# Grouping the scan's products of two slots, and reordering the work between two Mamba layers

## The chip, the cores and the metric

The kernel runs on one core of a Trainium2 chip. The metric is the device time of one launch in microseconds (us). A core has a matrix engine (TensorE, PE, with its weight loads as PEld), a vector engine (VectorE, DVE), a scalar engine for activations (ScalarE, ACT), a general engine (GpSimd, POOL), and a queue that issues the DMAs (SyncE, SP). Each engine works through its own list of instructions in order; semaphores tie the lists together.

## The reference

The network takes four images of 256 channels and 64 x 64 positions in float32 and applies four layers to each. The first two are recurrent and windowed attention layers, which the change does not touch. The third is a Mamba layer over the 4096 positions: a layer norm, a projection to 512 channels and a gate of 512, a causal convolution of four taps, SiLU, and then for each channel a state of 16 numbers that is carried along the sequence:

```python
def step(h, inp):
    d_t, u_t, B_t, C_t = inp
    dA = jnp.exp(d_t[..., None] * A)
    h = dA * h + (d_t * u_t)[..., None] * B_t[:, None, :]
    y_t = jnp.einsum('bdn,bn->bd', h, C_t)
    return (h, y_t)
```

After that come y + u * D, the gate silu(z), an output projection and a sum into x (with statistics of x that the next layer's norm uses). The fourth layer is a grouped Mamba: a layer norm over 256 channels, four groups of 64 channels that share one Mamba of 128 inner channels, a small MLP with GELU per group, a 1 x 1 convolution with batch norm, and SiLU; its result is added to x and written out.

## The kernel before, in words

The four images run one after the other: attention_layers, mamba_layer (the first Mamba layer) and grouped_mamba_layer (the second). The image x stays in SBUF.

Both Mamba layers use scan_blocks (L907). The sequence is cut into four chunks of 1024 positions (NC), and a chunk into four blocks of 128 channels, so there are 16 blocks. A block has 16 slots, one for each number n of the state, 256 slots per layer and image. For one slot i:

- spread (L937 to L951): PE copies row n of B over all 128 partitions into a PSUM tile pb (two bf16 matmuls of 512 columns against a picking column).
- L1019: DVE multiplies pb by du = delta * u, in place.
- decay (L954, L961): ACT computes da = exp(delta * a_n).
- L1025: DVE's scan instruction runs h = da * h + pb along the 1024 positions.
- L1031: POOL multiplies h by C (cb, loaded by DMA with a broadcast) into hc.
- turn (L969, L977): PE adds hc into y with eight transposes, which accumulate in PSUM over the 16 slots.

Some slots are "apart": n = 0, 5, 10 in the first layer, 0, 4, 8 in the second. There B is loaded by DMA (bb), POOL makes the product (L935), and ACT writes the exponentials into PSUM (dap). The tag pb has two PSUM buffers, which pb and dap take in turn, so what belongs to slot i + 2 can be written only when the scan of slot i has ended.

The order is written out by hand. For slot i the loop issues: the product of slot i, the scan, POOL's product of slot i + 2 if that is apart, hc, decay(i + 3), the loads, then background steps, spread(i + 2), further background steps (n + 0.5), turn(i - 1), and the exponentials of slot i + 2 if that is apart. Background steps come from a table per block (blk["bg"], filled by put): input projections (u_ps, z_ps), SiLUs, x_proj (tables of B and C), delta, norms, output projections and the MLP, each at a fixed slot. Each engine meets these in the order of issue. end (L985) finishes a block during the next one: a copy of y, transposes back, the D term (fin_ps), and the gate product (L991).

Between the layers, for each image (L1539 to L1587): a function center is called by scan_blocks after its last slot and ahead of the last turn. It computes the next norm's means (L1544) and subtracts them (L1548). Then follow the last output products (L1392), squares (L1561 and L863), sums over the channels (L1572 for the norm's variance, L817 for the statistics of x), a short chain on DVE, and the reciprocal root. In the second layer come the scaling, a first product, constants (skip, f1b, wf1, bns, bnb, L1923 to L1945), the folded convolution weights (folds, L1214, on the results of small matmuls at L1209), the first convolution on DVE (evict and convolve, L1895 to L1910), the SiLU of the first block, x_proj and delta, and then scan_blocks.

Of the kernel before, what the change touches and what calls it, by code (L numbers as in the profile page):

```python
# [8 lines left out]
F32 = mybir.dt.float32  # L9
# [3 lines left out]
ALU = mybir.AluOpType  # L13
# [5 lines left out]
P = 128  # L19
# [8 lines left out]
NT = 512  # L28
NC = 1024
# [15 lines left out]
class Net:  # L45
# [858 lines left out]

    def scan_blocks(self, blocks, loop, psum, psb, psy, apart, ends, first, last=None):  # L907
# [6 lines left out]

        def is_apart(i):
            return 0 < i < n_slot and slots[i][1] in apart

        def pieces(i):
            return halves if i == n_slot - 1 else [slice(0, NC)]
# [65 lines left out]
        def end(blk, n):  # L985
            if n == ends[0]:
                for ss in halves:
                    nc.scalar.activation(blk["du"][:, ss], blk["y"][:, ss], AF.Copy)
            for j, (ss, first) in enumerate(zip(halves, ends[1:])):
                if n == first + 1:  # L990
                    nc.vector.tensor_tensor(  # L991
                        blk["zs"][:, ss], blk["out", j], blk["zs"][:, ss], ALU.mult
                    )
# [21 lines left out]
            decay(i, True)  # L1015
            product(i)
        for i, (blk, n) in enumerate(slots):
            if not is_apart(i):
                nc.vector.tensor_tensor(pb[i], blk["du"], pb[i], ALU.mult)  # L1019
            h[i] = loop.tile([P, NC], F32, tag="h", name="h", bufs=3)  # L1020
            for ss in pieces(i):
                state = 0.0 if blk["first"] else blk["state"](n)
                if ss.start:
                    state = h[i][:, ss.start - 1 : ss.start]
                nc.vector.tensor_tensor_scan(  # L1025
                    h[i][:, ss], da[i][:, ss], pb[i][:, ss], state, ALU.mult, ALU.add
                )
# [12 lines left out]
            if i >= DS and n == ends[0]:  # L1040
                end(slots[i - DS][0], n)
            spread(i + 2)
            for step in blk["bg"].get(n + 0.5, ()):
                step()
            turn(i - 1)
            decay(i + 2, True)
            for d in (pb, da, cb):
                del d[i]
        if last:
            last()  # L1050
        turn(n_slot - 1)
        for n in range(ends[2] + 2):
            end(blocks[-1], n)


    def exp_ln_tables(self):
# [165 lines left out]
    def mamba_layer(self, x, bridge, pe_dram, w_in, w_cw, w_x, w_dt, w_out, v_dram):  # L1222
        tc, nc = self.tc, self.nc
        ND = 4
        with ExitStack() as ctx:
# [310 lines left out]
            xs3 = x.rearrange("p (c t) -> p c t", c=2)  # L1536


            def center():  # L1539
                nc.gpsimd.memset(xn[:, :, 0:3], 0.0)  # L1540
                pm = psb.tile([P, NC], F32, tag="pb", name="ln_pm")
                for ss in first:
                    for c in range(2):
                        nc.tensor.matmul(  # L1544
                            pm[:, ss], self.one_ln, xs3[:, c, ss], start=(c == 0), stop=(c == 1)
                        )
                for ss in first:
                    nc.vector.tensor_tensor(  # L1548
                        xn[:, :, 3 + ss.start : 3 + ss.stop], xs3[:, :, ss],
                        pm[:, ss].rearrange("p (o t) -> p o t", o=1).to_broadcast([P, 2, NT]),  # L1550
                        ALU.subtract,
                    )

            self.scan_blocks(
                [blk for c in chunks for blk in c["blocks"]], loop, psum, psb, psy, (0, 5, 10),
                (1, 2, 4), (xs0[4:6], (), xs0[6:]), center,
            )
            late_square, late_sums, late_squares, finish = late_stats
            sq3 = work.tile([P, 2, NC + 3], F32, tag="xn", name="ln_sq")
            for ss in first:  # L1560
# [5 lines left out]
            for s in range(2):  # L1566
                for m in range(2):
# [12 lines left out]
            wi = bridge.tile([P, 6, P], F32, tag="w2", name="m3_wi")  # L1580
            erow = self.eps_row(wi[:, 5, 0:S].rearrange("p (g t) -> p g t", t=2), finish())
# [22 lines left out]
    def grouped_mamba_layer(self, x, bridge, begun, ws_dram, outc_dram, v_dram, out_b, load):  # L1604
        tc, nc = self.tc, self.nc
        w_in, w_cw, w_x, w_dt, w_out, w_f1, w_f2 = ws_dram
        with ExitStack() as ctx:
# [136 lines left out]
            def delta(k, q):  # L1744
                return self.delta_steps(chunks[k]["blocks"][q], wdt, work, psum)
# [184 lines left out]
            f1b = wp.tile([P, 2], F32, name="m3_f1b")  # L1930
            pf = psum.tile([P, NT], F32, tag="mm", name="pf")
            for f in range(2):
                nc.tensor.matmul(
                    pf[:, f : f + 1], wf1[0:64, f * P : (f + 1) * P],
                    vec[0:64, M3_L1B : M3_L1B + 1], start=True, stop=True,
                )
            nc.vector.tensor_tensor(f1b, pf[:, 0:2], vec[:, M3_F1B : M3_F1B + 2], ALU.add)
            nc.vector.tensor_scalar(wf1, wf1, vec[:, M3_L1G : M3_L1G + 1], None, ALU.mult)
# [3 lines left out]
            nc.vector.tensor_tensor(bns, bns, vec[:, M3_BG : M3_BG + 2], ALU.mult)  # L1942
            bnb = wp.tile([P, 2], F32, name="m3_bnb")
            nc.vector.tensor_tensor(bnb, bns, vec[:, M3_BM : M3_BM + 2], ALU.mult)
            nc.vector.tensor_tensor(bnb, vec[:, M3_BB : M3_BB + 2], bnb, ALU.subtract)  # L1945
            for f in folds:
                f()
# [19 lines left out]
            for i, (k, c) in enumerate(pairs):  # L1967
                even, odd = chunks[k]["blocks"][2 * c : 2 * c + 2]

                def put(blk, where, steps):  # L1970
                    for i, f in zip(where, steps):
                        blk["bg"].setdefault(i, []).append(f)
# [7 lines left out]
                if more:  # L1980
# [5 lines left out]
                put(even, (4, 5, 9, 11, 12, 13), x_proj(k, 2 * c + 1))  # L1986
# [12 lines left out]
                put(even, (7, 9, 8, 9, 10), delta(k, 2 * c + 1))  # L1999
# [6 lines left out]
                put(even, (3,), (silu(k, c, "zs", also),))  # L2006
                if c == 1 and k:
                    put(even, (4, 5, 6, 7), [out(k - 1, *sm) for sm in outs])
                    put(even, (8,), [lambda k=k: load(slice((k - 1) * NC, k * NC))])
# [9 lines left out]
                    put(odd, (9, 11, 10, 11, 12), delta(nk, 2 * ncol))  # L2019
                    put(odd, (13, 14), [in_z(nk, ncol, s) for s in range(2)])  # L2020
            self.scan_blocks(
                [blk for c in chunks for blk in c["blocks"]], loop, psum, psb, psy, (0, 4, 8),
                (1, 2, 2), (xs0[2:4], (), xs0[4:]),
            )

# [161 lines left out]
```

## Time and profile before

| | us |
|---|---|
| median of three runs | 11817.76 |
| lowest and highest | 11803.92, 11832.72 |
| the profiled execution | 11811.95 |
| its span | 11810.1 |
| first Mamba loop, last image, first to last scan | 937 |
| between the layers, last image | 55 |
| second Mamba loop, last image | 956 |

| engine | busy share of the span |
|---|---|
| PE | 84% |
| DVE | 83% |
| POOL | 74% |
| ACT | 60% |

The span is cut from the profile's first to last instruction. Times on the timeline count from its start. In a line of the timeline the columns are start, length, engine, source line, operation, output <- inputs, shapes, and a count; in brackets stands the idle time ahead of the instruction and what ended it. Equal instructions that follow each other are merged. One 512-column float32 matmul leaves two records on PE.

### The profile page before, as it was taken

Reading aid. Unit: us, or ns where it says so; the run is one execution under the profiler, and the core shown is the slowest. Engines: PE = TensorE matmul, PEld = TensorE weight load, DVE = VectorE, ACT = ScalarE, POOL = GpSimd, SP = SyncE. Lnnn points to the kernel's source line nnn. Section 1 sums busy time; section 2 is a strip of 40 time slices with the busy share of each in tenths; the row PEclk is TensorE's granted clock in tenths of the full one; section 3 lists DMA queues with packets and bytes.
Section 4 is the critical chain, followed back from the end, with each engine's and each line's share of the span. In section 5 each row is a group of like instructions: output and inputs, shape, how many; then the busy total and the mean of one; then the engine's idle time right before and its main releaser. Section 6 shows DMA issues by size and latency. Waiting matters only on the chain. (4 is left out here: it accounts for less than half of the span.)

```text
span 11810.1 us, 191909 instructions
## 1 busy us (share of the span) xinstructions
PE 9965.7 (84%) x70632; PEld 5738.0 (49%) x71104; DVE 9804.7 (83%) x8342; ACT 7028.2 (60%) x13152; POOL 8773.6 (74%) x6070
## 2 busy tenths in 40 slices
PE   8998887777999888777799988877779998887777
PEld 4564554444456455444455645444435564544444
DVE  6678998998767799899876779989987678998998
ACT  4565555776456555577645655557764565555776
POOL 4666886898456688789745668868975566886897
PEclk9999998998999999899999989989999999998998
DMA  3354554454335455455433545545543354554554
GB/s 97 106 141 140 172 175 143 170 183 158 94 99 144 139 172 176 144 169 183 162 88 98 144 140 172 177 143 168 182 162 90 98 143 142 172 175 143 168 175 153
DMA packets 682507, 1742.11 MB, mean 148 GB/s; under 512 B 88896, under 2 KB 194896, under 8 KB 681312
## 3 DMA queue, kind: packets, MB, share of 16 engines
q1 hardware_dynamic: 676448, 1721.41, 45.3%
q8 instruction: 563, 9.22, 0.3%
q10 hardware_dynamic: 5120, 8.39, 0.3%
q14 instruction: 376, 3.08, 0.1%
HBM read 1601.52 MB, written 94.39 MB: 144 GB/s over the span
## 5 line engine op out<-in xcount | busy, mean ns | idle before, releaser
L1031 POOL TENSOR_TENSOR hc<-h,cb 128x1024 f32<-128x1024 f32 x2056 | 4808.6, 2350 | 794.5 <-DVE h L1025 345.2
L1025 DVE TENSOR_TENSOR_SCAN h<-da,m_state,pb 128x1024 f32<-128x1024 f32 x1248 | 2920.4, 2340 | 163.0 <-DVE pb L1019 1.9
L977 PE MATMUL y<-ident,hc 128*128 128x128 f32 x16384 | 2352.7, 291 | 446.4 <-POOL hc L1031 346.1
L977 PEld LDWEIGHTS y<-ident,hc 128*128 128x128 f32 x16384 | 2051.5, 151 | 1126.1 <-POOL hc L1031 573.0
L1019 DVE TENSOR_TENSOR pb<-du,pb 128x1024 f32<-128x1024 f32 x1672 | 2025.0, 1211 | 126.4 <-PE pb L949 103.9
L961 ACT ACTIVATE da<-delta,m_v 128x1024 f32<-128x1024 f32 x1672 | 1899.2, 1141 | 135.3 <-DVE h L1025 118.4
L949 PE MATMUL pb<-m_parts,pick 128*128 128x512 bf16 x2840 | 976.1, 414 | 842.0 <-DVE h L1025 772.6
L603 POOL TENSOR_SCALAR pr<-pr,sm,zero 128x256 f32<-128x256 f32 x2048 | 1107.2, 556 | 385.5 <-DVE sm L600 381.0
L588 ACT ACTIVATE pr<-sc,mn 128x256 f32<-128x256 f32 x2048 | 954.9, 478 | 515.7 <-DVE sm L600 399.1
L949 PEld LDWEIGHTS <-pick 128*128 128x128 bf16 x3312 | 263.7, 101 | 1788.1 <-DVE h L1025 976.7
L577 DVE TENSOR_REDUCE mn<-sc 128x4 f32<-128x1024 f32 x512 | 630.1, 1232 | 542.9 <-PE sc L565 542.8
L1025 DVE TENSOR_TENSOR_SCAN h<-da,pb 128x1024 f32<-128x1024 f32 x424 | 969.5, 2287 | 55.2 <-DVE pb L1019 1.0
L935 POOL TENSOR_TENSOR bb<-du,bb 128x1024 f32<-128x1024 f32 x376 | 888.3, 2363 | 118.1 <-DMA bb<-m_cd 110.1
L1025 DVE TENSOR_TENSOR_SCAN h<-dap,m_state,bb 128x1024 f32<-128x1024 f32 x288 | 672.3, 2334 | 66.7 <-ACT dap L961 48.7
L252 PE MATMUL conv_ps<-att_y,att_wb 128*128 128x512 f32 x1536 | 682.5, 594 | 0.0
L616 PE MATMUL pt_ps<-ident,pr 128*128 128x128 f32 x4096 | 637.9, 292 | 37.8 <-POOL pr L603 16.8
L565 PE MATMUL sc<-kv,q_swap 32*64 32x128 f32 x8192 | 594.5, 283 | 26.6 <-DMA kv<-kv_dram 9.8
L961 ACT ACTIVATE dap<-delta,m_v 128x1024 f32<-128x1024 f32 x376 | 419.7, 1116 | 314.6 <-DVE h L1025 239.3
L565 PE MATMUL sc<-kv,att_y 32*64 32x128 f32 x7168 | 577.1, 282 | 28.7 <-DMA kv<-kv_dram 22.9
L616 PEld LDWEIGHTS pt_ps<-ident,pr 128*128 128x128 f32 x4096 | 459.3, 146 | 165.6 <-POOL pr L603 108.4
L290 DVE SCALAR_TENSOR_TENSOR lp<-vimg,att_v,lp 128x512 f32<-128x512 f32 x672 | 507.7, 756 | 30.4 <-DVE lp L290 0.5
L565 PEld LDWEIGHTS sc<-kv,att_y 32*64 32x64 f32 x7168 | 428.1, 136 | 161.3 <-ACT pr L588 70.5
(303 smaller groups left out, 17818.2 us busy)
## 6 DMA issues: line engine op xcount, KB each, us to landing
cb<-m_cd SPq DMA_DIRECT2D x2048, 512.0 KB, 3.9
kv<-kv_dram SPq DMA_DIRECT2D x1984, 128.0 KB, 2.8
bb<-m_cd SPq DMA_DIRECT2D x376, 512.0 KB, 5.0
kv_dram<-kst SPq DMA_DIRECT2D x128, 256.0 KB, 3.4
kv_dram<-vn SPq DMA_DIRECT2D x128, 256.0 KB, 4.2
q_swap<-att_y SPq DMA_DIRECT2D x96, 256.0 KB, 4.3
m_pe<-in_pe_dram SPq DMA_DIRECT2D x32, 512.0 KB
out_dram<-yo SPq DMA_DIRECT2D x64, 256.0 KB, 2.0
```

The source lines that it names most:

```text
L252: nc.tensor.matmul(ps, w[:, k, w0 + m * P : w0 + (m + 1) * P], src[:, k], start=(k == 0), stop=(k == 1),)
L565: nc.tensor.matmul(sc[h][b * 64 : b * 64 + 64, r, w, m, :], (own(sj, m) if r == b else swap[sj % 2][:, m])[rows, 2 * a + w], kv[i, w][rows ...
L588: nc.scalar.activation(t[:, g].rearrange("p j r t -> p r j t"), sc[h][:, :, g // 2, g % 2, :].rearrange("p r (j t) -> p r j t", j=2), AF.E ...
L603: nc.gpsimd.tensor_scalar(t[:, g], t[:, g], s[:, g : g + 1], self.zero, ALU.mult, ALU.add)
L616: nc.tensor.transpose(pt[h][j][:, g, :], t[:, g, j].rearrange("p r t -> p (r t)"), self.ident,)
L935: nc.gpsimd.tensor_tensor(pb[i], slots[i][0]["du"], pb[i], ALU.mult)
L949: nc.tensor.matmul(pb[i][:, ss], self.pick[:, n : n + 1].to_broadcast([P, P]), blk["parts"][:, ss], start=True, stop=True,)
L961: nc.scalar.activation(da[i], blk["delta"], AF.Exp, scale=blk["a"](n))
L977: nc.tensor.matmul(blk["y"][:, ss], t[:, ss], self.ident, is_transpose=True, start=(n == 0 and ss.start % NT == 0), stop=(n == DS - 1 and ...
L1019: nc.vector.tensor_tensor(pb[i], blk["du"], pb[i], ALU.mult)
L1025: nc.vector.tensor_tensor_scan(h[i][:, ss], da[i][:, ss], pb[i][:, ss], state, ALU.mult, ALU.add)
L1031: nc.gpsimd.tensor_tensor(hc[i][:, ss], h[i][:, ss], cb[i][:, ss], ALU.mult)
```

## The change

In scan_blocks, a new argument twos names slots: n = 2, 4, 7, 9, 12, 14 in the first layer and 2, 6, 10, 12, 14 in the second. Where the next slot is one of these, the product of the next slot is issued directly behind that of this slot, and both scans come after. There turn(i - 1) is also issued ahead of spread(i + 2) and no longer after it. The first slots of each layer (i up to 4) stay as they were.

Between the layers, center is split into halves: the last turn comes first, and the means and subtractions are issued in between the steps that finish the last block. The squares of the second half, and the variance sums (now behind the sums of x's statistics), move back.

In the second layer, f1b, wf1, bns and bnb move behind the first delta; x_proj of the first block is issued ahead of the eviction of the second one; the four folds become background steps of the first block (slots 12 to 15); and in the first block alone the SiLU group moves from slot 3 to 5, x_proj's first two steps from 4 and 5 to 6 and 7, and the delta steps from (7, 9, 8, 9, 10) to (9, 10, 10, 11, 11).

The diff, cut to its core:

```diff
+        def with_next(i):
+            return 4 < i < n_slot - 1 and slots[i + 1][1] in twos
+
+        def times_du(i):
+            if not is_apart(i):
+                nc.vector.tensor_tensor(pb[i], slots[i][0]["du"], pb[i], ALU.mult)
...
         for i, (blk, n) in enumerate(slots):
-            if not is_apart(i):
-                nc.vector.tensor_tensor(pb[i], blk["du"], pb[i], ALU.mult)
+            if not (i and with_next(i - 1)):
+                times_du(i)
+            if with_next(i):
+                times_du(i + 1)
...
+            if with_next(i):
+                turn(i - 1)
             spread(i + 2)
             for step in blk["bg"].get(n + 0.5, ()):
                 step()
-            turn(i - 1)
+            if not with_next(i):
+                turn(i - 1)
             decay(i + 2, True)
...
-        if last:
-            last()
         turn(n_slot - 1)
         for n in range(ends[2] + 2):
             end(blocks[-1], n)
+            for f in last.get(n, ()):
+                f()
...
-                (1, 2, 4), (xs0[4:6], (), xs0[6:]), center,
+                (1, 2, 4), (xs0[4:6], (), xs0[6:]),
+                {1: [lambda: mean3(0)], 2: [lambda: center(0)], 4: [lambda: mean3(1)],
+                 5: [lambda: center(1)]},
             )
...
             for s in range(2):
+                if s == 0:
+                    square3(first[0])
                 for m in range(2):
                     for f in out_proj(n_chunk - 1, s, m, ((ND - 1,),), False):
                         f()
                 late_square(s, sq)
+            square3(first[1])
+            for f in (late_sums, lambda s: late_squares(s, sq)):
+                for s in range(2):
+                    f(s)
+            for s in range(2):
                 for c in range(2):
                     nc.tensor.matmul(
                         pv[:, first[s]], self.one_ln, sq3[:, c, first[s]], start=(c == 0),
                         stop=False,
                     )
-            for s in range(2):
-                late_sums(s)
-                late_squares(s, sq)
...
             self.exp_ln_tables()
+            xs0, ds0 = x_proj(0, 0), delta(0, 0)
+            for f in xs0[:2]:
+                f()
             for s in range(2):
                 evict(1, s)
                 convolve(1, s)
-            xs0, ds0 = x_proj(0, 0), delta(0, 0)
-            for f in (*xs0[:2], *ds0[:4], lambda: ds0[4](nc.vector)):
+            for f in (*ds0[:4], lambda: ds0[4](nc.vector)):
                 f()
...
+                if i == 0:
+                    put(even, (12, 13, 14, 15), folds)
+                put(even, (3 if i else 5,), (silu(k, c, "zs", also),))
```

More of the change, by code (lines that the diff above doesn't have):

```diff
@@ L896, in col_stats, with scan_blocks @@
         )
-    def scan_blocks(self, blocks, loop, psum, psb, psy, apart, ends, first, last=None):
+    def scan_blocks(self, blocks, loop, psum, psb, psy, apart, twos, ends, first, last={}):
         nc = self.nc
@@ L1536, in mamba_layer, with mean3, center @@
             xs3 = x.rearrange("p (c t) -> p c t", c=2)
[L1539 to L1551, printed above, removed]
-                    )
+            box3 = {}
+            def mean3(s):
+                if s == 0:
+                    nc.gpsimd.memset(xn[:, :, 0:3], 0.0)
+                    box3["pm"] = psb.tile([P, NC], F32, tag="pb", name="ln_pm")
+                for c in range(2):
+                    nc.tensor.matmul(
+                        box3["pm"][:, first[s]], self.one_ln, xs3[:, c, first[s]],
+                        start=(c == 0), stop=(c == 1),
+                    )
+            def center(s):
+                ss = first[s]
+                nc.vector.tensor_tensor(
+                    xn[:, :, 3 + ss.start : 3 + ss.stop], xs3[:, :, ss],
+                    box3["pm"][:, ss].rearrange("p (o t) -> p o t", o=1).to_broadcast([P, 2, NT]),
+                    ALU.subtract,
+                )
             self.scan_blocks(
-                [blk for c in chunks for blk in c["blocks"]], loop, psum, psb, psy, (0, 5, 10),
-                (1, 2, 4), (xs0[4:6], (), xs0[6:]), center,
+                [blk for c in chunks for blk in c["blocks"]], loop, psum, psb, psy, (0, 5, 10), (2, 4, 7, 9, 12, 14),
+                (1, 2, 4), (xs0[4:6], (), xs0[6:]),
+                {1: [lambda: mean3(0)], 2: [lambda: center(0)], 4: [lambda: mean3(1)],
+                 5: [lambda: center(1)]},
             )
@@ L1559, in mamba_layer, with square3 @@
             sq3 = work.tile([P, 2, NC + 3], F32, tag="xn", name="ln_sq")
-            for ss in first:
+            def square3(ss):
                 nc.scalar.activation(
@@ L1566, in mamba_layer @@
             for s in range(2):
+                if s == 0:
+                    square3(first[0])
                 for m in range(2):
@@ L1928, in grouped_mamba_layer @@
             nc.vector.tensor_scalar(wout, wout, wm, None, ALU.add)
[L1930 to L1938, printed above, removed]
             bns = wp.tile([P, 2], F32, name="m3_bns")
             self.rsqrt(bns, vec[:, M3_BV : M3_BV + 2], self.eps)
[L1942 to L1947, printed above, removed]
             for c in chunks:
@@ L1961, in grouped_mamba_layer @@
                 convolve(1, s)
-            xs0, ds0 = x_proj(0, 0), delta(0, 0)
-            for f in (*xs0[:2], *ds0[:4], lambda: ds0[4](nc.vector)):
-                f()
+            for f in (*ds0[:4], lambda: ds0[4](nc.vector)):
+                f()
+            f1b = wp.tile([P, 2], F32, name="m3_f1b")
+            pf = psum.tile([P, NT], F32, tag="mm", name="pf")
+            for f in range(2):
+                nc.tensor.matmul(
+                    pf[:, f : f + 1], wf1[0:64, f * P : (f + 1) * P],
+                    vec[0:64, M3_L1B : M3_L1B + 1], start=True, stop=True,
+                )
+            nc.vector.tensor_tensor(f1b, pf[:, 0:2], vec[:, M3_F1B : M3_F1B + 2], ALU.add)
+            nc.vector.tensor_scalar(wf1, wf1, vec[:, M3_L1G : M3_L1G + 1], None, ALU.mult)
+            nc.vector.tensor_tensor(bns, bns, vec[:, M3_BG : M3_BG + 2], ALU.mult)
+            bnb = wp.tile([P, 2], F32, name="m3_bnb")
+            nc.vector.tensor_tensor(bnb, bns, vec[:, M3_BM : M3_BM + 2], ALU.mult)
+            nc.vector.tensor_tensor(bnb, vec[:, M3_BB : M3_BB + 2], bnb, ALU.subtract)
             pairs = [(k, c) for k in range(n_chunk) for c in range(2)]
@@ L1985, in grouped_mamba_layer @@
                     put(odd, (1, 2, 3), h1[2:])
-                put(even, (4, 5, 9, 11, 12, 13), x_proj(k, 2 * c + 1))
+                put(even, (4, 5, 9, 11, 12, 13) if i else (6, 7, 9, 11, 12, 13), x_proj(k, 2 * c + 1))
                 if i:
@@ L1998, in grouped_mamba_layer @@
                         put(odd, (3, 4, 4.5, 5, 6), m1[3:])
-                put(even, (7, 9, 8, 9, 10), delta(k, 2 * c + 1))
+                put(even, (7, 9, 8, 9, 10) if i else (9, 10, 10, 11, 11), delta(k, 2 * c + 1))
                 also = [lambda k=k: out_silu(k - 1)] if c == 1 and k else []
@@ L2005, in grouped_mamba_layer @@
                     also = [lambda blk=odd: silu_of(blk, "u")]
-                put(even, (3,), (silu(k, c, "zs", also),))
+                if i == 0:
+                    put(even, (12, 13, 14, 15), folds)
+                put(even, (3 if i else 5,), (silu(k, c, "zs", also),))
                 if c == 1 and k:
@@ L2021, in grouped_mamba_layer @@
             self.scan_blocks(
-                [blk for c in chunks for blk in c["blocks"]], loop, psum, psb, psy, (0, 4, 8),
+                [blk for c in chunks for blk in c["blocks"]], loop, psum, psb, psy, (0, 4, 8), (2, 6, 10, 12, 14),
                 (1, 2, 2), (xs0[2:4], (), xs0[4:]),
```

## The prediction

> **What bounds the kernel now.** I read the page's busy shares first, then a table of stretches cut at the scan loops, the timeline of VectorE (DVE) inside a loop, the list of waits, and the timeline of TensorE (PE) where it is fullest. The page alone does not decide it: PE is busy 84%, DVE 83%, POOL 74%. The stretches do. For the last of the four images (loop of the first Mamba layer, the time between the layers, loop of the second):
>
> ```profile
> 9826.00:10763.00 937.00, 800.64 (x3459) 463.73 (x3519) 878.41 (x544) 510.38 (x746) 798.15 (x353) 0.94 0.52 174
> 10763.00:10818.00 55.00, 45.40 (x105) 20.55 (x104) 27.51 (x52) 24.41 (x36) 2.33 (x4) 0.75 0.09 32
> 10818.00:11774.00 956.00, 734.85 (x3429) 405.30 (x3486) 873.52 (x531) 662.58 (x959) 852.02 (x387) 0.91 0.51 171
> ```
>
> The columns are length, then PE, weight loads, DVE, ACT, POOL, the granted clock, DMA. DVE is busy 878 of 937 us and 874 of 956 us, the fullest engine in both loops. They are 4 x (937 + 956) = 7572 us of the 11810. The rest of DVE's time there is of two kinds. The first shows when the loop runs smoothly:
>
> ```profile
> 11098.76 2.35 DVE L1025 TENSOR_TENSOR_SCAN h<-da,m_state,pb 128x1024 f32<-128x1024 f32 x1
> 11101.02 1.21 DVE L1019 TENSOR_TENSOR pb<-du,pb 128x1024 f32<-128x1024 f32 x1
> 11102.36 2.35 DVE L1025 TENSOR_TENSOR_SCAN h<-da,m_state,pb 128x1024 f32<-128x1024 f32 x1
> ...
> 11130.21 2.35 DVE L1025 TENSOR_TENSOR_SCAN h<-da,m_state,pb 128x1024 f32<-128x1024 f32 x1
> 11132.47 1.26 DVE L991 TENSOR_TENSOR m_zs<-fin_ps,m_zs 128x512 f32<-128x512 f32 x2
> ```
>
> A slot takes 3.60 us. The product starts 0.09 us before the scan ahead of it has ended (11098.76 + 2.35 = 11101.11), and so does L991 after its scan; but the scan that reads the product starts 0.13 us after it (11101.02 + 1.21 = 11102.23). The second kind is waiting for other engines (total us, times, longest, whole run):
>
> ```profile
> DVE pb L1019 <- PE pb L949: 103.9, 86, 5.5
> DVE delta L1156 <- ACT delta L1152: 103.9, 78, 8.8
> ...
> DVE h L1025 <- ACT dap L961: 75.0, 45, 2.9
> ```
>
> **The change, part by part: pairs of products.** The new instruction order has 173 pairs per image (94 in the first Mamba layer, 79 in the second), 692 in all: product, product, scan, scan. Two slots now have boundaries +0.13, -0.09, +0.13, -0.09, which is +0.08. In a pair no instruction reads its direct predecessor: four times -0.085, which is -0.34. Saving 0.42 to 0.43 us a pair, so 173 x 0.43 = 74 us per image, if the second product's input is there in time.
>
> Here a rule of the Trainium skill speaks against the change. "VectorE: DVE Perf Modes", section "The DRAIN you can't avoid", says that each DVE operation is followed by a pipeline flush which chaining without semaphores doesn't avoid, and that waits between operations cost nothing extra. By that rule regrouping saves 0. The rows differ: 0.13 us where the next instruction reads the result, -0.09 us where it does not, in the same loop. I take the rows; the rule's sum stays as a rival.
>
> The price is in the new wait. The products are read from two PSUM buffers, so slot j+1's copy (L949) can only be spread by PE once scan j-1 has freed its buffer. Before, product j and scan j (3.5 us) lay between that and the need. Now only product j does: need comes 1.21 - 2 x 0.085 = 1.04 us after scan j-1, and behind the waiting product are both scans of the pair, hence POOL's hc and the transposes. What PE needs:
>
> ```profile
> 10463.08 1.88 PE L1339 MATMUL z_ps<-m_xn,m_wz 128*128 128x512 f32 x4
> 10464.12 2.35 DVE L1025 TENSOR_TENSOR_SCAN h<-da,m_state,pb 128x1024 f32<-128x1024 f32 x1 [0.49 <-DVE pb L1019]
> 10464.80 1.88 PE L1314 MATMUL u_ps<-m_xn,m_wxi_w 128*128 128x512 f32 x4
> 10466.52 0.59 PE L949 MATMUL pb<-m_parts,pick 128*128 128x512 bf16 x2
> 10466.95 1.04 PE L977 MATMUL y<-ident,hc 128*128 128x128 f32 x8
> 10467.15 1.23 DVE L1019 TENSOR_TENSOR pb<-du,pb 128x1024 f32<-128x1024 f32 x1 [0.68 <-PE pb L949]
> ```
>
> Scan end 10466.47, spread 10466.52, product 10467.15: 0.05 us to react, 0.63 us from spread to product. By the starts, four records of 512 columns cost 1.72 us (0.86 per matmul of two records), a spread 0.43, a slot's eight transposes 0.87; pairs of 64-row matmuls of the second layer run side by side and cost about half. Almost every pair follows a scan that ran directly after another scan (2.27 us apart). So with W the PE work queued between the spreads of slots j and j+1, the second product waits W - (2.27 + 1.04 - 0.63 - 0.48) = W - 2.2 us, less 0.67 us where a delta or gate step stands on DVE ahead of the pair. Moving the transposes of slot j-1 ahead of the spread takes 0.87 us out of W in successive pairs. From the new PE order I priced W for every pair of the last image. In the first layer 58 of 94 are on time, 12 wait up to 0.43 us, 24 more (largest 2.1, where W is 4.3: transposes, z and u); sum 35 us. In the second 48 of 79 are on time, 22 lose more than they gain; sum 27 us. That is 62 us per image against 74.
>
> Not all of it is new: the 103.9 us of today, 26 per image, are waits at the same bursts of PE, and PE's work is unchanged. I count those once: 74 - 62 + 26 = 38 us saved per image, 152 us in all. Bounds: nothing waits, 74 x 4 = 298 us saved; waits twice as long, 74 - 124 + 26 = -24, 96 us lost. The central value is nearest to the rows, since it prices PE by its own spacings; but it has PE begin each burst without a backlog. ACT's exponentials into those buffers (dap, 1.12 us) lose cover in the same way at n = 5 and 10 of the first layer, where 75.0 / 4 = 19 us per image are waited today for all n; I leave that wait unchanged, within 8 us per image either way.
>
> A second rule bears on W: "TensorE: Matmul & The Clock Gate", section "Part 1: The HAM clock gate", halves the clock after an idle window of about 3.4 us. After 3.22 us idle at 10478.12 the four z records at 10480.66 take 3.51 us, not 1.88. Pairs bunch PE's work, and where a pair has only two spreads and two transposes (2.6 of 6.8 us) PE idles 4 us. The rows' warm prices leave 62 us; by the rule the bursts of the four light blocks at the end of the first layer would double, W of 2.6 turning into some 4.5, about +12 us per image. I keep the warm price, as their PE is busy 72 to 87% today.
>
> **Between the layers and at the start of the second.**
>
> ```profile
> 10763.87 5.28 PE L1544 MATMUL ln_pm<-x,one_ln 128*128 128x512 f32 x8
> 10768.99 1.04 PE L977 MATMUL y<-ident,hc 128*128 128x128 f32 x8
> ```
>
> The last transposes stand behind the means for 5 us. Put first, they end some 4.6 us earlier. The means then take 1.7 us each inside the finish, the second one ahead of the output products, so the gate products gain 3.7 us but the first output product only 1.9. The eight variance records behind the sums leave the middle and lie at the end of PE's row of matmuls, 3.4 us: the epsilon matmuls (10788.75 today) start about 3.2 us earlier, since PE is then the chain. Folds, f1b and bnb leave DVE ahead of the convolution, which waits for PE there (1.77 and 0.58 us): 2.6 us earlier; f1b, wf1, bns and bnb come back behind du at 1.0 us. The folds cost 4 x 0.29 us in slots 12 to 15. The SiLU group (5.5 us on ACT, with two table loads) makes slot 6 wait 4.56 us for its spread; two slots later most of that hides behind two scans: 4 us. The moved x_proj puts its two DMAs to m_cd behind two cb loads on SP and du one slot later on POOL; both have a block's worth of cover, I price them at 0; uncovered, du is 2.4 us. Sum 3.2 + 2.6 - 1.0 - 1.2 + 4 = 7.6, taken as 8 us per image (2 to 12): 32 us.
>
> **Sum.** 11811.95 (profiled execution, span 11810.1) - 152 - 32 = 11628. The median shown is 5.8 us above that execution: 11634.
>
> **Rivals.** *Full pairs* (0.17): PE is ready nearly always, as the transposes moved forward free it earlier. Speaks for it: PE has 136 us idle in the first loop. Against: 46 priced pairs per image exceed their own gain. About 11818 - 298 - 32 = 11490. *Only the layer boundary* (0.10): the skill's rule holds, or waits eat the pairs exactly: 11818 - 32 = 11786. *The second product starves the scan* (0.15), the case on the slow side: PE enters each burst with a backlog, as its 801 of 937 us suggest, at slots 2, 6 and 12 above all. The place is L1019's second product in front of two scans; it decides from a mean wait of (74 + 26 + 8) / 173 = 0.62 us per pair, against 0.36 priced. Doubled, 125 us per image: 11818 + 96 - 32 = 11882. *Partial gain*, the forecast (0.58): 11540 to 11750.
>
> **How the numbers follow.** Measurement tells about 0.2% (24 us) from no change. Faster: the first, second and last case nearly whole, minus a rest of boundary-only and partial near zero: 0.77; same 0.08; slower 0.15. The range 11510 to 11830 leaves out part of the full case and most of the starving one.
>
> **What would show it.** In the profile after: scans of a pair 2.27 us apart with product, product ahead, and L1025's idle after L1019 gone in pairs (right) or still 0.13 (the rule). Waits of L1019 for L949: about 62 us per image at second products, against 26; above 108 the forecast's sign fails. The stretch between the layers: 55 down to about 50. The 4.56 us at slot 6 gone. Wrong if ACT's dap, not PE, becomes the releaser after pairs, or if POOL (852 of 956 us in the second loop) holds the transposes that now stand ahead of the spreads.

## The result and the profile after

The changed kernel takes 12294.29 us (median of 4; 12270.93 to 12305.76) against 11812.92 us before (4 runs): ratio 1.0405, 95% interval 1.0392 to 1.0418. It is 4.05% slower. The profiled execution has a span of 12292.9 us.

The stretches of the last image, cut as before (length, PE, weight loads, DVE, ACT, POOL, granted clock, DMA):

```profile
10195.00:11186.00 991.00, 834.39 (x3518) 473.34 (x3519) 864.16 (x543) 512.85 (x746) 795.82 (x353) 0.92 0.48 164
11187.00:11239.00 52.00, 39.53 (x92) 16.87 (x92) 26.16 (x48) 26.77 (x38) 3.00 (x3) 0.80 0.14 53
11239.00:12257.00 1018.00, 769.99 (x3496) 416.19 (x3496) 862.15 (x535) 664.08 (x957) 849.93 (x387) 0.89 0.47 159
```

The loops went from 937 and 956 us to 991 and 1018. DVE is busy less than before (864 and 862 us against 878 and 874): it waits more.

What the pairs were meant to do is there. DVE's timeline near the end of the first layer's loop, where nothing is late:

```profile
11117.47 2.33 DVE L923 TENSOR_TENSOR pb<-du,pb 128x1024 f32<-128x1024 f32 x2
11119.71 4.58 DVE L1034 TENSOR_TENSOR_SCAN h<-da,m_state,pb 128x1024 f32<-128x1024 f32 x2
11124.20 1.21 DVE L923 TENSOR_TENSOR pb<-du,pb 128x1024 f32<-128x1024 f32 x1
```

Two products, two scans and the next product follow each other with each start ahead of the last end (11117.47 + 2.33 = 11119.80, the scans start at 11119.71; they end at 11124.29, the product starts at 11124.20). The pair takes 6.73 us, against 2 x 3.60. DVE's list of waits (total us, times, longest) shows the price:

```profile
DVE pb L923 <- PE pb L956: 917.7, 511, 5.9
...
DVE h L1034 <- ACT dap L968: 60.9, 28, 3.8
DVE delta L1168 <- ACT delta L1164: 58.9, 46, 8.8
```

The product (now L923) waits 917.7 us for its spread (now L956), where it was 103.9; the waits for ACT have become smaller. PE's own list:

```profile
PE y L984 <- POOL hc L1040: 696.2, 520, 4.0
PE pb L956 <- DVE h L1034: 515.3, 508, 3.7
```

The same two lines of the kernel before:

```profile
PE pb L949 <- DVE h L1025: 772.6, 493, 5.5
PE y L977 <- POOL hc L1031: 346.1, 277, 3.8
```

PE waits 696.2 us at the transposes (now L984) for POOL's hc (before: 346.1), and 515.3 us at the spread for a scan (before: 772.6). It stands ready at the spread for less time; instead the spread is late, and DVE waits.

One such place, in the second layer, with what stands between two spreads:

```profile
11610.57 2.35 DVE L1034 TENSOR_TENSOR_SCAN h<-da,m_state,pb 128x1024 f32<-128x1024 f32 x1
11610.61 2.35 POOL L942 TENSOR_TENSOR bb<-du,bb 128x1024 f32<-128x1024 f32 x1
...
11613.00 2.35 DVE L1034 TENSOR_TENSOR_SCAN h<-dap,m_state,bb 128x1024 f32<-128x1024 f32 x1
11613.35 0.59 PE L956 MATMUL pb<-m_parts,pick 128*128 128x512 bf16 x2
...
11615.27 1.21 DVE L923 TENSOR_TENSOR pb<-du,pb 128x1024 f32<-128x1024 f32 x1
...
11615.33 1.09 PE L984 MATMUL y<-ident,hc 128*128 128x128 f32 x8 [1.39 <-POOL hc L1040]
...
11616.26 1.88 PE L1851 MATMUL oc_ps<-xo,m_woc 128*128 128x512 f32 x4
...
11617.98 1.88 PE L1096 MATMUL ln_pm<-x,one_ln 128*128 128x512 f32 x4
...
11619.69 0.59 PE L956 MATMUL pb<-m_parts,pick 128*128 128x512 bf16 x2
...
11620.33 1.23 DVE L923 TENSOR_TENSOR pb<-du,pb 128x1024 f32<-128x1024 f32 x1 [3.85 <-PE pb L956]
```

By the prediction's rule this pair waits 4.3 - 2.2 = 2.1 us (W: transposes 0.87, two groups of four records 1.72 each). It waited 3.85. The first spread itself came 0.38 us late (at 11613.35; the scan that freed its buffer had ended at 11612.92, and 0.05 us is the usual reaction), and inside W the transposes waited 1.39 us for hc, since POOL still had an apart product (L942) ahead of it. 2.1 + 0.38 + 1.39 = 3.87 us is the wait.

### The profile page after: what moved, and what is told of

It is laid out like the page before. It is cut to its first block, busy times and chain, and to the rows that moved or that the text cites. A ratio compares the mean times of both kernels' runs of the same rounds, so it can differ in the third digit from the quotient of the medians.

```text
span 12292.9 us, 193673 instructions
## 1 busy us (share of the span) xinstructions
PE 10275.8 (84%) x71104; PEld 5834.9 (47%) x71104; DVE 9703.7 (79%) x8342; ACT 7053.0 (57%) x13152; POOL 8762.4 (71%) x6070
## 5 line engine op out<-in xcount | busy, mean ns | idle before, releaser
L984 PE MATMUL y<-ident,hc 128*128 128x128 f32 x16384 | 2430.9, 298 | 865.9 <-POOL hc L1040 696.2
L984 PEld LDWEIGHTS y<-ident,hc 128*128 128x128 f32 x16384 | 2073.6, 154 | 1784.6 <-POOL hc L1040 1272.9
L1034 DVE TENSOR_TENSOR_SCAN h<-da,m_state,pb 128x1024 f32<-128x1024 f32 x1248 | 2872.6, 2329 | 26.2 <-ACT m_state L973 0.5
L923 DVE TENSOR_TENSOR pb<-du,pb 128x1024 f32<-128x1024 f32 x1672 | 2013.7, 1218 | 924.4 <-PE pb L956 917.7
L956 PE MATMUL pb<-m_parts,pick 128*128 128x512 bf16 x3312 | 1115.5, 422 | 563.7 <-DVE h L1034 515.3
L942 POOL TENSOR_TENSOR bb<-du,bb 128x1024 f32<-128x1024 f32 x376 | 887.2, 2360 | 25.1 <-DMA bb<-m_cd 24.9
L956 PEld LDWEIGHTS <-pick 128*128 128x128 bf16 x3312 | 280.1, 103 | 1311.1 <-DVE h L1034 696.2
```

The lines of the kernel that those rows point to most:

```text
L923: nc.vector.tensor_tensor(pb[i], slots[i][0]["du"], pb[i], ALU.mult)
L942: nc.gpsimd.tensor_tensor(pb[i], slots[i][0]["du"], pb[i], ALU.mult)
L956: nc.tensor.matmul(pb[i][:, ss], self.pick[:, n : n + 1].to_broadcast([P, P]), blk["parts"][:, ss], start=True, stop=True,)
L984: nc.tensor.matmul(blk["y"][:, ss], t[:, ss], self.ident, is_transpose=True, start=(n == 0 and ss.start % NT == 0), stop=(n == DS - 1 and ...
L1034: nc.vector.tensor_tensor_scan(h[i][:, ss], da[i][:, ss], pb[i][:, ss], state, ALU.mult, ALU.add)
```

## The experiments

All gaps between neighbouring DVE instructions of both loops, taken from the traces and averaged over the four images, make one table for the readings below (us per image; "small" is the sum of all gaps under 0.2 us, which the pairs were to shrink; "second" are waits of a second product in a pair; "other" is all other gaps over 0.2 us).

| kernel | loops | small | second | other |
|---|---|---|---|---|
| boundary part alone | 935.6 + 944.6 | 6.1 | 0 | 77 |
| changed kernel | 991.6 + 1015.7 | -60.3 | 193.6 | 78 |
| transposes ready, pairs | 962.2 + 994.9 | -60.3 | 152.2 | 71 |
| transposes ready, no pairs | 922.6 + 933.5 | 4.7 | 0 | 54 |
| half the transposes, pairs | 977.3 + 1021.8 | -60.9 | 155.3 | 110 |
| half the transposes, no pairs | 923.1 + 951.9 | 6.0 | 0 | 71 |
| second spread first, pairs | 956.5 + 973.9 | -59.9 | 20.7 | 173 |
| that order, no pairs | 967.9 + 983.6 | 8.6 | 0 | 144 |

**The two parts apart.** The kernel before with the new twos, times_du and turn order alone; and the changed kernel with empty twos:

```diff
-  (0, 5, 10), (2, 4, 7, 9, 12, 14),
+  (0, 5, 10), (),
-  (0, 4, 8), (2, 6, 10, 12, 14),
+  (0, 4, 8), (),
```

> The kernel before with the pairs of products and the moved transposes alone; everything between the layers and at the start of the second layer as before. All theories that put the loss into the pairs expect the whole of it here: 12290 to 12330 us, with L919 to L923's products waiting about 900 us for their spreads. If the loss came from the start of the second layer or from the boundary, this would stay below 11900.

> The changed kernel with no pairs at all (both lists of slots empty). The forecast's own terms give 32 us less than before, 11780; the profile after shows only 4 us of gain in the four stretches between the layers, so that, with a few us at slot 6 of the second layer, I expect 11780 to 11810. Above 11830 the boundary would be part of the loss.

Pairs alone: 12337.46 us, ratio 1.0458 (1.0441 to 1.0476). Boundary alone: 11774.01 us, 0.9971 (0.9963 to 0.9979). The first is just above the expected 12290 to 12330, the second just below 11780 to 11810. The loss is all in the pairs, 520 us between the changed kernel and the boundary alone.

**Where the transposes stand.** turn(i - 1) behind the spread everywhere, as before the change; and turn(i - 2) at the head of each slot's background, so that hc has a slot more:

```diff
-            if with_next(i):
-                turn(i - 1)
             spread(i + 2)
...
-            if not with_next(i):
-                turn(i - 1)
+            turn(i - 1)
```

```diff
             load_b(i + 4)
+            turn(i - 2)
...
-            if with_next(i):
-                turn(i - 1)
             spread(i + 2)
...
-            if not with_next(i):
-                turn(i - 1)
```

> The changed kernel with the transposes of slot i - 1 behind the spread of slot i + 2 in every slot, as before the change. Theory 'the moved transposes': a spread now stands behind POOL's hc; put back, the wait of the products falls by half or more, to 12000 or less. Theory 'POOL is late anyway' (the transposes that were not moved hold the work in front of the second spread): little changes, 12250 to 12350. Theory 'PE has too much work between two spreads': slower than the changed kernel, 12300 to 12450, since 0.87 us more stands between the spreads of successive pairs.

> The changed kernel with its pairs, but with the transposes of slot i - 2 at the head of slot i's background work, in place of those of slot i - 1 behind or ahead of the spread. Nothing is left out. POOL has a slot longer for hc, and the first transposes of a block no longer wait for the copy of y. Theory 'transposes held by POOL': as with ready transposes or better, 11950 to 12080. Theory 'only PE's work counts': no better than the changed kernel, 12230 to 12350, since as many transposes stand between two spreads as before.

12295.13 us (1.0427; 1.0409 to 1.0445) and 12286.95 us (1.0409; 1.0393 to 1.0424): no change beside 12294.29. In the first of them PE waited 405 us for hc instead of 696, and the second products' waits grew from 194 to 217 us per image all the same. That the transposes stand ahead of the spread is not the cause.

**Transposes that never wait.** They read a constant in place of hc, with and without pairs; C's part of y is left out in both.

```diff
-                        blk["y"][:, ss], t[:, ss], self.ident, is_transpose=True,
+                        blk["y"][:, ss], self.one_ln, self.ident, is_transpose=True,
```

> The changed kernel in which the eight transposes of a slot read a constant tile and not hc, so the multiplication by C is left out of y, while PE runs as many transposes in the same places and POOL still makes hc. The transposes then never wait for POOL. Theory 'POOL's hc holds the transposes, and these hold the second spread': the wait of the products falls from 918 us to the 250 to 350 that PE's work alone was priced at, and the time to 11600 to 11800. Theory 'PE's own work between the spreads, with its backlog': the wait stays above 750 us and the time above 12150.

> The kernel of the run with the boundary alone (no pairs), with transposes that read a constant tile, so that C is left out of y as in the run with ready transposes. It is that run's control. Without pairs the spreads have 3.5 us of cover, so POOL's lateness should cost little: 11700 to 11775. Then the pairs cost some 270 to 340 us even when no transpose waits for POOL, and that part must be PE's own work and backlog. If instead it comes to 11500 or less, the transposes' waiting costs the kernel without pairs as well, and the share that I give to it in the pairs is too large.

With pairs 12043.3 us (1.0207; 1.019 to 1.0224), between what the two theories gave; without 11633.47 us (0.9848; 0.9833 to 0.9863), below the expected range. The waiting for hc costs the kernel without pairs as well: 141 us (11774 less 11633), against 251 with pairs. The pairs still cost 410 us. So POOL's hold on the transposes bears about 110 of the 520 us, or 90 by the ratios, since the runs with and without pairs stem from different batches.

**Only the pairs that were on time.** The 65 pairs per image whose second product did not wait in the changed kernel's trace, named by slot number.

```diff
-            return 4 < i < n_slot - 1 and slots[i + 1][1] in twos
+            return 4 < i < n_slot - 1 and i + 1 in twos
```

> The changed kernel with pairs only where the trace of the changed kernel shows the second product on time in all four images: 41 of 94 slots in the first layer, 24 of 79 in the second. If the loss is the wait of second products and nothing else, each of the 65 pairs keeps its 0.43 us: 4 x 65 x 0.43 = 112 us less than the run with the boundary alone (11774), 11660 to 11710. If pairs also cost elsewhere (POOL and ACT fed in bursts), 11750 or more.

11759.66 us (0.9954; 0.9941 to 0.9968). The DVE gaps show the gain, 24 us per image, and 17 us of waits at second products that had been on time, 5 us elsewhere. Of these 17 us, 14 lie at pairs whose neighbour two slots earlier had been dropped. Slots 120 and 121 of the first layer in the last image, in the changed kernel:

```profile
10671.25 0.61 PE L956 MATMUL pb<-m_parts,pick 128*128 128x512 bf16 x2
10671.70 1.88 PE L1379 MATMUL x_ps<-m_u,m_wx 128*128 128x512 f32 x4
10673.49 0.60 PE L956 MATMUL pb<-m_parts,pick 128*128 128x512 bf16 x2
```

and here, without the pair at 119:

```profile
10253.33 0.59 PE L956 MATMUL pb<-m_parts,pick 128*128 128x512 bf16 x2
10253.76 1.04 PE L984 MATMUL y<-ident,hc 128*128 128x128 f32 x8
10254.63 1.88 PE L1379 MATMUL x_ps<-m_u,m_wx 128*128 128x512 f32 x4
10256.35 0.59 PE L956 MATMUL pb<-m_parts,pick 128*128 128x512 bf16 x2
```

Two things had kept such pairs on time. Where the earlier pair is gone, its slot's eight transposes stand behind the spread again and fall between these two (the time from the first spread to the second is 2.29 us in the changed kernel and 3.46 here, mean of the 59 waits of this kind in the four images). And PE arrives later: the first spread started 0.46 us after its release there and 2.39 here, presumably since the earlier pair's own wait had let PE catch up. So the list of on-time pairs of one trace can't be added up: the expected 11660 to 11710 was wrong.

**Products into SBUF.** In the second layer the product leaves PSUM for a tile of its own (two buffers), which frees the spread's buffer a scan earlier; cb and da have three buffers there instead of four.

```diff
-                nc.vector.tensor_tensor(pb[i], slots[i][0]["du"], pb[i], ALU.mult)
+                out = pb[i]
+                if apart == (0, 4, 8):
+                    out = loop.tile([P, NC], F32, tag="pr", name="pr", bufs=2)
+                nc.vector.tensor_tensor(out, slots[i][0]["du"], pb[i], ALU.mult)
+                pb[i] = out
```

> The changed kernel in which the second layer's products are written to two SBUF tiles and not back into PSUM; to find the space, cb and da have three buffers there and not four. A PSUM buffer is then free once its product is made, not once its scan has run. Theory 'the two PSUM buffers make the wait': second products of the second layer find their spreads, and its loop falls from 1018 us to 920 to 960: 11950 to 12080 in all, the first layer unchanged at about 992. Against it: the scans then read two tiles of SBUF, and the Trainium skill ('GPSIMD Engine Reference', section '1. Specifications') names contention between POOL and DVE instructions with two SBUF inputs; then hc and the scans of the second layer grow beyond 2.35 us and the loop stays above 1000.

13527.26 us (1.1462; 1.1445 to 1.148). The theory that the buffers make the wait is not decided, since what had been named against it came true: the second layer's loop took 1325 us. The groups of DVE by form:

```profile
L1038 DVE TENSOR_TENSOR_SCAN h<-da,m_state,pr 128x1024 f32<-128x1024 f32 x620 | 1908.0, 3102 | 19.1 <-ACT m_state L977 0.5 <-DVE pr L926 0.5
L1038 DVE TENSOR_TENSOR_SCAN h<-da,m_state,pb 128x1024 f32<-128x1024 f32 x620 | 1428.8, 2333 | 6.2 <-DVE pb L926 0.5
```

The scan with both inputs in SBUF takes 3102 ns, with one in PSUM 2333 ns, and POOL's hc slows down with it (mean over both layers 2611 ns, 2356 in the changed kernel). PE then waits 1614.9 us at the transposes for hc, and the second layer's second products wait 163 us per image and not 98, although their buffers are free a scan earlier.

**Less work on PE.** The transposes of the states 1, 2, 5, 6, 9, 10, 13, 14 are left out (those states are missing from y), with pairs and without.

```diff
                 t = hc.pop(i)
+                if n % 4 in (1, 2):
+                    return
```

> The changed kernel with its pairs, but the transposes of the states 1, 2, 5, 6, 9, 10, 13 and 14 of every block left out (so those states are missing from y): PE has some 8 x 0.9 us less per block, in the first loop about 115 of 834 busy us. Theory 'PE's load between the spreads': against the same kernel without pairs the pairs cost at most a fifth of the 520 us that they cost with all transposes, or gain; 11400 to 11750 us. Theory 'the rhythm of the scans, ACT and POOL': the cost stays above 300 us; 11950 us or more.

> Control of the run with half of the transposes: the same states left out of y, no pairs. Both theories: between the 11633 us of the kernel whose transposes never wait and the 11774 us of the boundary part alone, near 11650 us.

With pairs 12268.4 us (1.0379; 1.0362 to 1.0396), without 11754.28 us (0.9947; 0.993 to 0.9964). The pairs cost 514 us, as with all transposes. The theory of PE's load between the spreads was wrong as stated, and the number is the one that the rival, the rhythm of the scans, ACT and POOL, gave. PE's timeline of the kernel with pairs at the longest wait of a second product (5.5 us, state 14 of the second layer):

```profile
11771.45 1.04 PE L956 MATMUL pb<-m_parts,pick 128*128 128x512 bf16 x2 [3.58 <-DVE h L1036]
11772.42 2.08 PE L1803 MATMUL f_ps<-m_sq,m_wf 64*128 64x512 f32 x4
11775.27 2.08 PE L1828 MATMUL f_ps<-m_xn,m_skip 128*128 128x512 f32 x2 [0.77 <-ACT hid L1810]
11777.27 1.98 PE L1833 MATMUL f_ps<-hid,m_wf 128*64 128x512 f32 x4
11779.18 1.03 PE L956 MATMUL pb<-m_parts,pick 128*128 128x512 bf16 x2
...
11781.11 1.08 PE L1833 MATMUL f_ps<-hid,m_wf 128*64 128x512 f32 x4
```

Ten records of the MLP stand between the spreads, and they run at half speed after 3.58 us of idling: four of them take 1.98 us here and 1.08 us at 11781.11. In this kernel 24% (first layer) and 40% (second) of the transposes follow each other by more than 0.16 us (full speed is 0.11), against 14% and 24% in the changed kernel and 10% and 18% before. The control without pairs has 21% and 29%. So part of the freed time went into slower matmuls, and the run separates neither load from clock nor load from rhythm.

**The second spread first.** In the slot ahead of a pair's second slot, the spread goes ahead of the slot's background and transposes; nothing is left out. The control has this order and no pairs.

```diff
+            if with_next(i + 1):
+                spread(i + 2)
             if i >= DS and n != ends[0]:
                 end(slots[i - DS][0], n)
...
-            spread(i + 2)
+            if not with_next(i + 1):
+                spread(i + 2)
```

```diff
-            if not (i and with_next(i - 1)):
-                times_du(i)
-            if with_next(i):
-                times_du(i + 1)
+            times_du(i)
```

> Nothing is left out: the spread of a pair's second product stands ahead of the background matmuls and the transposes of its slot in PE's order, with nothing but the half-slot steps between it and the spread before. Theory 'the place in the queue': the 186 to 196 us per image of second products' waits (fourfold some 760 us) vanish and the pairs earn their 0.09 and 0.13 us gaps; 11480 to 11750 us. Theory 'PE is in order and has the work to do, so waits only move': PE now stands before that spread until the scan ends and has the slot's background behind it; second products' waits fall below 60 us per image, but those of first and single products, of the scans for the state product and of y for x_ps grow by as much or more; 12150 to 12500 us, PE's wait for the scans at the spread above the 515 us of the changed kernel.

> Nothing is left out: the order of the run with the second spreads first, at the same slots, but no product is issued ahead of its scan, so there are no pairs. Theory 'the 105 us per image of waits that were left there at first products come from PE standing at the spread with its slot's work behind it': those waits stay (above 60 us per image) and the time is above 11850 us. Theory 'they come from the pair, which delays the scan that releases the next spread': they go back to the 26 us per image of the boundary part alone and the time is 11700 to 11800 us.

With pairs 11979.64 us (1.0145; 1.0128 to 1.0162), between what the two theories gave; without 12066.13 us (1.0215; 1.0201 to 1.023). DVE's line for the products with pairs (of all products), PE's for the spreads in that order without pairs, and the same in the boundary part alone:

```profile
DVE pb L923 <- PE pb L956: 396.2, 255, 4.4
```

```profile
PE pb L956 <- DVE h L1031: 931.1, 618, 5.3
```

```profile
PE pb L956 <- DVE h L1034: 760.6, 497, 5.5
```

The second products' waits fall from 194 to 21 us per image: where their spread stands in PE's order decides over them. In exchange the other waits grow from 78 to 173, mostly at first and single products, whose spreads now have two slots' background ahead of them. The control shows that this is mostly the price of the order: without pairs they are 144, and the order alone costs 292 us (12066 less 11774), with PE standing 931.1 us at the spread (760.6 in the boundary part alone) while its background waits behind. In that order the pairs do gain, by 0.70% or some 83 us, of 274 us (4 x 68.5) by which they shrink the small gaps.

**A few pairs in that order.** Pairs at n = 2, 7, 12 in the first layer and 10 in the second, 63 per image.

```diff
-  (0, 5, 10), (2, 4, 7, 9, 12, 14),
+  (0, 5, 10), (2, 7, 12),
-  (0, 4, 8), (2, 6, 10, 12, 14),
+  (0, 4, 8), (10,),
```

> Nothing is left out: the spread-first order, with pairs only at states 2, 7 and 12 in the first layer and 10 in the second (96 to 64 per image in all instead of 173), which are the pairs whose own unit was shorter by 1.6 to 6.8 us per image than without pairs in the run before this one, and which have a single slot behind them. Theory 'a pair pays where its second spread stands first and a single slot follows in which PE catches up': 62 pairs per image at 0.43 us, 27 us per image, some 105 in all, less what moves; 11670 to 11760 us against 11774 of the boundary part alone. Theory 'whatever a pair gains comes back as a wait elsewhere': 11774 us or more.

11837.29 us (1.0019; 1.0009 to 1.0029): a miss, as the second theory had it. The small gaps shrink by 24 us per image, the waits grow by 37. I had picked these pairs by the length of their own units in the run before; what they delay seems to lie elsewhere, which was not followed up. No version with pairs beat the boundary part by an amount that these runs tell apart: the 65 pairs gave 0.9954 (to 0.9968), the boundary alone 0.9971 (from 0.9963), in different batches.

## Why the prediction was wrong

The sum of the pairs, term by term, in us per image (changed kernel less boundary part alone):

| term | predicted | measured |
|---|---|---|
| boundaries of the pairs | -74 | -66 |
| waits of second products | +62 | +194 |
| all other waits (predicted: today's at the products, counted once) | -26 | +1 |
| sum | -38 | +129 |

Four times 129 is 516 of the 520 us.

*The gain* was right. In pairs the starts lie 0.09 us ahead of the end, and the small gaps fell by 66 us. The prediction had set these rows against the Trainium skill, "VectorE: DVE Perf Modes", section "The DRAIN you can't avoid". That section, though, also says that a next operation which is not held starts earlier, and the independent neighbours here agree; that regrouping saves 0 was more than it states.

*The step that failed* is the price of the second product's wait. The mechanism was named rightly (the spread, released by scan j - 1, behind W on PE) and so was its threshold: the mean wait at second products is 194 / 173 = 1.12 us, above the 0.62 from which the rival "the second product starves the scan" decides. The term that failed is its size, 62 us per image predicted and 194 measured. In the last image 120 of 173 second spreads started over 0.3 us after their release. For these 120 I compared W by the prediction's prices with the trace:

- The first spread of the pair was late itself: 91 us. The prediction said that it priced PE "without a backlog", and then took the central value all the same.
- W took 452 us and not 296. Of the 156 us more, PE was idle for 76: 61 ahead of transposes, for hc most of all, the rest ahead of the steps that read ACT's or DVE's results (x_ps, f_ps and the norms). The page before had shown that wait, 346.1 us at the transposes for hc, and none of it was put into W.
- The other 80 us is PE running slower than the prices of warm, merged rows: half-speed records and the switches between groups. Some 38 us of it lie between neighbouring equal records (transposes, spreads, 128-row matmuls) that start at about twice their warm distance, 21 of them between transposes; the rest, mostly at the switches, I can't split. Slow records belonged in the price, though at other places than the prediction had looked for them by the clock rule (the Trainium skill, "TensorE: Matmul & The Clock Gate", section "Part 1: The HAM clock gate"): only 1 us of the 38 lies in the four light blocks, which it had weighed at 12 us and left out.

Not all of these 247 us became waits; some went into the slack that W left.

*Counting today's waits once* was right in part. Of the 26.0 us at products in the boundary part, 16.3 sit at products that are second ones in the changed kernel, and are in the 194 there. But the first and single products, which wait 9.7 us in the boundary part, wait 35.8 us in the changed kernel, 23.5 of it at state 3 of the second layer (1.4 before), in the slot behind a pair. The prediction had no term for waits outside the pairs; why they arise there was not tested. Taken together, the waits at products rose by 203 us per image and not by 36, and all waits elsewhere fell by 8.

*Why the orders that were tried don't repair it.* The runs that put the spread first and its control show the conflict. PE has background for each slot, and with two PSUM buffers it can do it only while it isn't needed at a spread. If it does the background first, the second product waits (194 us per image). If it goes to the spread first, it stands there until the scan ends, and the next products wait (an order that alone costs 292 us). Without pairs the need comes a product and a scan (3.5 us) after the release, and PE fits the background in. With pairs it comes 1.04 us after. That the place of the spread in PE's order moves the waits from the second products to the first and single ones is shown by these two runs; which share of the 292 us is PE's idling and which its clock stays open, and so does what a third buffer would do: no run has one, and the way through SBUF made the scan slower.

*Rivals.* "Full pairs", "partial gain" and "only the layer boundary" fell. "The second product starves the scan" has the direction, the place and the backlog, but at 11882 it was 412 us short. POOL as the holder of the transposes, named as a way to be wrong, bears 90 to 110 of the 520 us. ACT's dap did not become the releaser (75.0 us before, 60.9 after).

*The boundary part* was right in sum: 36 us measured (11810.51 of the kernel before beside it, less 11774.01), 32 predicted. Its places were partly others, so the fit of the sum is in part luck. Per image, 0.9 us lie in the stretch between the layers (53.1 us, mean of four images, to 52.2), where 4.8 were to come off; 5.2 in the first block of the second layer, where slot 6's wait (4.3 to 5.5 us) is gone in every image (4 predicted, less 1.2 for the folds); and some 3 behind it, for which there was no term.

## What to carry to other kernels

When an instruction is moved closer to the event that frees its input's buffer, price what the producing engine has queued between two such events by its real rows, waits and clock included, and with the lateness with which it arrives; here a 0.4 us gain per pair did not pay for a need that comes 2.5 us earlier on an engine that works in order and is 84% busy. A list of places that were on time in one trace doesn't carry over, because what stood around them, its waits and its order, had kept them on time. Repairing one order with another needs a control with the new order alone: here it cost more than the pairs had to give.

## What had not been expected of the hardware

A scan of 128x1024 with both inputs in SBUF took 3102 ns, with one of them in PSUM 2333 ns, and POOL's 128x1024 multiplies slowed down beside it (hc 2356 to 2611 ns over both layers, the apart product 2360 to 2942 ns). With the transposes of 8 of 16 states left out, the granted clock of the execution fell from 0.919 to 0.875 (without pairs from 0.938 to 0.890), and the remaining matmuls took longer (the transposes' mean went from 298 to 319 ns): the waits of the second products only fell from 194 to 155 us per image.
